# Four transformer-like layers on one core: operands of the scan's last batch, the order of two products, and where small steps are issued

## The chip, the cores and the metric

One core of one Trainium2 chip. The metric is the device time of one execution in microseconds (us). The engines are PE (matmul; its weight loads are shown as PEld), DVE (VectorE), ACT (ScalarE), POOL (GpSimd) and SP (SyncE, which here issues DMAs). Each takes its own instructions in order, and so do the DMA queues of SP, ACT and POOL in issuing.

## The reference, cut to what matters

The input is x of 4 batches x 512 tokens x 512 features, float32. Four layers follow each other, each added to x: causal attention, a ternary-weight FFN, a selective state-space scan, and a block of latent attention with a mixture of experts. The change touches the second stage (only in time: what runs between its products), the third, and the beginning of the fourth:

```python
# third layer, on the normed x; r = 128, n = 16 states, D = 512 features
xz = jnp.einsum('btd,rd->btr', x, W_xproj)
delta_r, B_mat, C_mat = xz[..., :r], xz[..., r:r + n], xz[..., r + n:]
delta = jax.nn.softplus(jnp.einsum('btr,dr->btd', delta_r, W_dt) + b_dt)
dA = jnp.exp(delta[..., None] * -jnp.exp(A_log))
Bu = delta[..., None] * B_mat[:, :, None, :] * x[..., None]
def step(h, inp):
    dA_t, Bu_t, C_t = inp
    h = dA_t * h + Bu_t
    return h, jnp.sum(h * C_t[:, None, :], axis=-1)
# fourth layer: the rmsnorm's weights ln1_w multiply the inputs of these three projections
kv_d, q_d, k_r = x @ kv_d_w, x @ q_d_w, x @ rope_k_w
```

## The kernel before, in words

The kernel goes through five stages: the first attention, the FFN (batches b = 0 to 3, eleven blocks f of hidden features each), the scan, the second attention, and the experts. Work of the next stage is cut into pieces by Python generators, and each `yield` ends a piece; the loop of the running stage calls `next` at fixed places, so the pieces lie between its own instructions.

**FFN.** PE's order is the order of the code; the other engines' order is set by a planner. `gated` (L819) makes the two hidden products of a block into a pair tile `pg` (two PSUM banks), ACT and DVE turn it into `sil`, `gh` and `gl`, and `down` (L837) multiplies back. Three pieces are called in each block, one of them between the two products of `gated`. In batches 1 to 3 these are pieces of `prepare(b - 1)`, which makes the inputs of the scan for the batch before: the projections `drT`, B and C, then in two halves the products with W_dt into a pair tile `pz` (L606), of which ACT takes the absolute value (`e`, L607) and DVE the positive part (`delta`, L608); then exponential, logarithm and sums, the store of `delta` to `deltas` and of delta times x, turned, to `dxs`, both in DRAM. Pair tiles have two buffers, single banks four.

**Scan.** Here the order of all five engines is the order of the code. There are 128 steps m over (batch, state n, half of the features), 32 steps a batch. In a step: `scale` (each second step) loads `diag` by SP and makes, by ACT, three rows `bu` (L1016) and four `da` (L1022) for the state after; `turn` brings the inputs into PSUM by PE (L1029, L1034) for the step after; `scan` is two DVE scans (L1042) into `h` (three buffers); `weigh` loads `cb` (L1050, three buffers) and POOL multiplies, `hc` (L1053); `add_up` sums three steps later on PE (L1066). `finish` adds a batch's sums to x at the third step of the batch after.

The scan's own inputs `delta_l` and `dxT` lie in the pool `large`, two buffers each, filled from DRAM by `fetch`: four pairs of SP loads, one pair a step. The inputs of the last batch are prepared during the scan by `prepare_last`, called at the first three steps and then at each second one; its tiles lie in a pool `c_p` on the right side of SBUF. It ends with, for each of four blocks k of features, ACT's copy of the product `pd` to `delta` (L738), its store to `deltas` (L739, ACT's queue), DVE's product with x (`ux`, L741), PE's turn `tpd` (L751), ACT's copy `st` (L734) and its store to `dxs` (L735, ACT's queue). The first block's copy is at step 67; at step 84 what is left is done at once, `c_p` is closed, and the pools `far` and `d_w` are opened in its place. Their first users at step 84 are SP's loads of `ln2` (L1121), `wr` (L1125) and `br` (L1127) and POOL's memset of `wr` (L1124). From step 84 `fetch(3)` loads the last batch, from 88 one weight of the second attention is loaded a step (eleven, L1134), and at steps 100, 102, 104 and 106 POOL multiplies a quarter of `wlat` and `wrk` by the norm's factors `ln1` (L1164; the profile calls wrk's tile `w_b`). Meanwhile `enter(0)` runs at every third step from 86: statistics of x by DVE (86 to 95), `shifted` and squares by ACT (L155, L915; 98 to 107), `root_inverse` (`ri_ln`, `ri_rms`: DVE L102, then POOL L103; 95 and 107), and rows and turns (110 to 125).

Of the kernel before, what the change touches and what calls it, by code (L numbers as in the profile page):

```python
# [11 lines left out]
F32 = mybir.dt.float32  # L12
# [3 lines left out]
ALU = mybir.AluOpType  # L16
# [30 lines left out]
def block_kernel(ctx: ExitStack, tc: tile.TileContext, a: dict, out: bass.AP):  # L47
# [24 lines left out]
    def by_tokens(x, b):  # L72
        return x[b * T : (b + 1) * T, :].rearrange("(t p) c -> p t c", p=P)

    def by_rows(w):
        return w.rearrange("(k p) o -> p k o", p=P)
# [420 lines left out]
    large = scans.enter_context(tc.tile_pool(name="large", bufs=2, reuse_waits="tile"))  # L497
    loaded = {}

    def fetch(b):  # L500

        delta = large.tile([P, NK, T], F32, tag="one", name="delta_l")
        dxT = large.tile([P, NT, C], F32, tag="two", name="dxT")
        loaded[b] = delta, dxT
        for i in range(NT):
            nc.sync.dma_start(dxT[:, i, :], by_tokens(dxs, b)[:, i, :])
            nc.sync.dma_start(delta[:, i, :], by_rows(deltas[b])[:, i, :])
            yield
# [45 lines left out]
    def prepare(b, pool, spot, spots, ahead):  # L554


        x = xs[b]
        uT = pool.tile([P, NK, T], F32, tag="uT", name="uT")
        ops, rows = [], {}
        layer_norm(pool, x, lambda t, op: ops.append(op))  # L560
        yield

        def make(t):
            row = rows[t] = pool.tile([P, C], F32, tag="row", name="row_s", bufs=ahead)
            ops[t](row)
            ud = pool.tile([P, C], F32, tag="u", name="ud")
            nc.gpsimd.tensor_tensor(ud, row, dpar, ALU.mult)
            nc.gpsimd.tensor_tensor(x[:, t, :], x[:, t, :], ud, ALU.add)

        make(0)  # L570
        make(1)
        yield
        for t in range(NT):
            transpose_into(uT, rows.pop(t), t * P, spot=spot)
            if t == 1:
                make(2)
                make(3)
            yield
        pd = spot("pd")
        for k in range(NK):  # L580
            nc.tensor.matmul(pd, wx[:, k, :RANK], uT[:, k, :], start=k == 0, stop=k == NK - 1)
            if k == 1:
                yield
        drT = pool.tile([P, T], F32, tag="drT", name="drT")
        nc.scalar.copy(drT, pd)
        yield
        pb = spot("pb")
        latents(pb, uT)
        bcT = pool.tile([P, P], F32, tag="bcT", name="bcT")
        nc.scalar.copy(bcT, pb[:, :P])  # L590
        keep_latents(b, bcT, nc.sync)
        yield
        pb = spot("pbt")
        nc.tensor.transpose(pb[:, :P], bcT, ident)
        e = pool.tile([P, NK, T], F32, tag="e", name="diag_s")
        nc.sync.dma_start(diags[b], keep_inputs(b, pb, e))
        yield
        yield


        delta = pool.tile([P, NK, T], F32, tag="delta", name="delta")
        e = pool.tile([P, NK, T], F32, tag="e", name="e")
        for half in range(2):
            for i, pz in enumerate(spots("pz")):
                k = 2 * half + i
                nc.tensor.matmul(pz, wdt[:, k * P : (k + 1) * P], drT, start=True, stop=True)  # L606
                nc.scalar.activation(e[:, k, :], pz, AF.Abs, bias=bdt[:, k : k + 1])  # L607
                nc.vector.tensor_scalar(delta[:, k, :], pz, bdt[:, k : k + 1], 0.0, ALU.add, ALU.max)  # L608
            yield half == 1
        nc.scalar.activation(e, e, AF.Exp, scale=-1.0)  # L610
        yield True
        for k in range(NK):
            u = pool.tile([P, T], F32, tag="u", name="u")
            nc.vector.tensor_scalar(u, e[:, k, :], 1.0, -1.0, ALU.add, ALU.add)
            nc.vector.tensor_tensor(u, e[:, k, :], u, ALU.subtract)
            nc.vector.tensor_tensor(delta[:, k, :], delta[:, k, :], u, ALU.add)
            yield True
        nc.scalar.activation(e, e, AF.Ln, bias=1.0)
        yield True
        scaled = {}  # L620

        def finish(k):
            nc.vector.tensor_tensor(delta[:, k, :], delta[:, k, :], e[:, k, :], ALU.add)
            nc.sync.dma_start(deltas[b, k * P : (k + 1) * P, :], delta[:, k, :])
            scaled[k] = pool.tile([P, T], F32, tag="ux", name="ux", bufs=2)
            nc.vector.tensor_tensor(scaled[k], delta[:, k, :], uT[:, k, :], ALU.mult)

        def turn_out(k):
            tp, ux = spot("tpd"), scaled.pop(k)
            for t in range(NT):  # L630
                nc.tensor.transpose(tp[:, t * P : (t + 1) * P], ux[:, t * P : (t + 1) * P], ident)
            st = pool.tile([P, NT, P], F32, tag="st", name="st")
            nc.scalar.copy(st.rearrange("p t q -> p (t q)"), tp)
            nc.sync.dma_start(by_tokens(dxs, b)[:, :, k * P : (k + 1) * P], st)

        finish(0)
        yield True
        finish(1)
        yield
        for k in range(NK):  # L640
            turn_out(k)
            if k + 2 < NK:
                yield True
                finish(k + 2)
            yield

    def prepare_last(b, pool):
# [70 lines left out]
        for t in range(NT + 1):  # L718
            if t > 0:
                nc.vector.tensor_tensor(x[:, t - 1, :], x[:, t - 1, :], y, ALU.add)  # L720
            if t < NT:
                y = bank("du")
                for k in range(NK):
                    nc.tensor.matmul(
                        y[:, k * P : (k + 1) * P], uT[:, k, t * P : (t + 1) * P], dd[:, k, :],
                        start=True, stop=True,
                    )
                yield
        terms = ((ident, relu), (ident, e), (minus, over), (ident, ln))
        scaled = tp = None  # L730
        for k in range(NK + 2):
            if k >= 2:
                st = pool.tile([P, NT, P], F32, tag="st", name="st")
                nc.scalar.copy(st.rearrange("p t q -> p (t q)"), tp)  # L734
                nc.scalar.dma_start(by_tokens(dxs, b)[:, :, (k - 2) * P : (k - 1) * P], st)  # L735
            if 1 <= k <= NK:
                delta = pool.tile([P, T], F32, tag="delta", name="delta", bufs=2)
                nc.scalar.copy(delta, pd)  # L738
                nc.scalar.dma_start(deltas[b, (k - 1) * P : k * P, :], delta)  # L739
                scaled = pool.tile([P, T], F32, tag="ux", name="ux", bufs=2)  # L740
                nc.vector.tensor_tensor(scaled, pd, uT[:, k - 1, :], ALU.mult)  # L741
            if k < NK:
                pd = bank("pdl")
                for i, (w, term) in enumerate(terms):
                    nc.tensor.matmul(pd, w, term[:, k, :], start=i == 0, stop=i == 3)
                    if i % 2 == 0:
                        yield
            if 1 <= k <= NK:
                tp = bank("tpd")
                for t in range(NT):  # L750
                    nc.tensor.transpose(tp[:, t * P : (t + 1) * P], scaled[:, t * P : (t + 1) * P], ident)  # L751
                yield
# [244 lines left out]
    with tc.tile_pool(name="c_1", bufs=1, reuse_waits="tile") as c1, tc.tile_pool(  # L997
# [83 lines left out]
        with tc.manual_schedule(engines=engines):  # L1081
# [4 lines left out]
            for m, (b, n, half) in enumerate(steps):  # L1086
# [27 lines left out]
                if m == 84:  # L1114
# [3 lines left out]

                    far = ctx.enter_context(tc.tile_pool(name="far", bufs=1, side="right"))
                    ln2 = far.tile([P, C], F32, tag="ln2", name="ln2")  # L1120
                    nc.sync.dma_start(ln2, a["ln2_w"].partition_broadcast(P))  # L1121

                    wr = far.tile([P, NK, RW], F32, tag="wr", name="wr")
                    nc.gpsimd.memset(wr, 0.0)  # L1124
                    nc.sync.dma_start(wr[:, :, :NR], by_rows(a["router_w"]))  # L1125
                    br = far.tile([P, NR], F32, tag="br", name="br")
                    nc.sync.dma_start(br, a["router_b"].partition_broadcast(P))  # L1127
                    logit = far.tile([P, TT, NR], F32, tag="logit", name="logit")

                    hs = [far.tile([P, NT, C], F32, tag=f"h{b}", name=f"h{b}") for b in range(B)]  # L1130
# [22 lines left out]
                    cos1 = held("cos1", [P, NT, RD], a["cos1"].rearrange("(t p) d -> p t d", p=P))  # L1153
                    sin1 = held("sin1", [P, NT, RD], a["sin1"].rearrange("(t p) d -> p t d", p=P))
                    wow = held("wow", [P, NK, C], by_rows(a["o_w"]))
                    coming = fetch(B - 1)
                if m >= 84:
                    next(coming, None)
                if m >= 88 and loads:
                    loads.pop(0)()  # L1160
                if 100 <= m < 100 + 2 * NK and m % 2 == 0:
                    k = (m - 100) // 2
                    for w in (wlat[:, k].rearrange("p i r -> p (i r)"), wrk[:, k]):
                        nc.gpsimd.tensor_scalar(w, w, ln1[:, k : k + 1], None, ALU.mult)  # L1164
            for step in steps[-3:]:
                add_up(*step)
            finish(B - 1)
# [569 lines left out]
```

## Time and profile before

| | us |
|---|---|
| median of 3 runs | 1910.6 (1908.81 to 1911.85) |
| profiled execution | 1912.04 |
| its span, first to last instruction | 1910.3 |
| mean granted TensorE clock | 0.980 |
| FFN, about | 480 to 753 |
| scan, first to last scan instruction | 755.3 to 1109.1 |

In the profile a line names engine, line of the kernel, operation and tiles (written <- read). Times are counted from the first instruction. An entry in brackets at the end of a timeline line is the idle time of the engine before it and what ended that; a group's last numbers are busy time and the mean of one in ns. One step of the scan starts its POOL product at 757.7 us (step 0), 985.65 (84), 1032.7 (98) and 1111.6 (127).

### The profile page before, as it was taken

What the parts mean: (1) busy time and instruction counts of PE and PEld (TensorE: products, weight loads), DVE (VectorE), ACT (ScalarE), POOL (GpSimd) and SP (SyncE); (2) the same over time, 40 slices, a digit from 0 to 9 for tenths busy, and PEclk for the clock granted to TensorE, in tenths of its full rate; (3) what the DMA queues carried; (4) which work ended last, traced back from release to release, by engine and by line L of the source; (5) the groups of instructions that cost most, each with busy time, mean ns of one, the idle gap of its engine ahead of it and who ended that gap; (6) DMA issues with size and microseconds to landing.
All of it is one profiled execution on the core that took longest, in us unless ns stands there. A gap on an engine that the chain in (4) does not pass through costs nothing. (4 is left out here: it accounts for less than half of the span.)

```text
span 1910.3 us, 27470 instructions
## 1 busy us (share of the span) xinstructions
PE 1767.4 (93%) x10374; PEld 1089.5 (57%) x10374; DVE 1119.4 (59%) x1812; ACT 937.5 (49%) x1932; POOL 575.0 (30%) x391
## 2 busy tenths in 40 slices
PE   7999999999999988988988888999999999999998
PEld 3433343437766666878877764555555554554444
DVE  6456445656564636998979856475565663422222
ACT  2433433333242436989977956566676662111111
POOL 2221212120202020989868940100001000144431
PEclk9999999999999999999999988999999999999999
DMA  7002200102010202332234200000001005545545
GB/s 250 8 1 89 82 1 1 45 1 78 1 56 34 89 23 78 96 112 81 70 127 125 62 6 1 1 10 14 1 23 34 23 7 179 196 89 89 93 81 139
DMA packets 78470, 119.27 MB, mean 62 GB/s; under 512 B 9802, under 2 KB 37066, under 8 KB 77780
## 3 DMA queue, kind: packets, MB, share of 16 engines
q1 hardware_dynamic: 66148, 92.97, 15.1%
q0 software_dynamic: 8656, 20.32, 6.0%
q10 hardware_dynamic: 3536, 4.23, 0.7%
q8 instruction: 83, 1.36, 0.3%
q14 instruction: 47, 0.39, 0.1%
HBM read 85.12 MB, written 35.52 MB: 63 GB/s over the span
## 5 line engine op out<-in xcount | busy, mean ns | idle before, releaser
L1053 POOL TENSOR_TENSOR hc<-h,cb 128x1024 f32<-128x1024 f32 x128 | 301.1, 2406 | 112.6 <-DVE h L1042 94.1
L1042 DVE TENSOR_TENSOR_SCAN h<-da,bu 128x512 f32<-128x512 f32 x256 | 291.2, 1199 | 26.1 <-PE bu L1034 13.1
L284 PE MATMUL pq<-wqkv,hT 128*128 128x512 f32 x384 | 179.4, 615 | 1.8 <-ACT hT L133 1.8
L1022 ACT ACTIVATE da<-delta_l,am 128x511 f32<-128x511 f32 x256 | 163.9, 709 | 6.7 <-DVE h L1042 6.7
L1314 ACT ACTIVATE pr<-scd,nm 128x128 f32<-128x128 f32 (+3 forms) x256 | 133.2, 528 | 56.1 <-DVE nm L1311 53.5
L819 PE MATMUL pg<-hTh,w 128*128 128x512 f32 (+1 forms) x352 | 146.3, 416 | 2.4 <-DVE sil L825 1.7
L1066 PE MATMUL ys<-ident,hc 128*128 128x128 f32 x1024 | 138.6, 279 | 6.9 <-POOL hc L1053 4.0
L819 PE MATMUL pg<-hTl,w 128*128 128x512 f32 (+1 forms) x352 | 140.1, 398 | 0.2 <-DVE hTl L807 0.2
L1034 PE MATMUL bu<-ident,bu 128*128 128x128 f32 x768 | 133.2, 281 | 7.5 <-ACT bu L1016 7.5
L1616 PE MATMUL pgr<-wgu,gTe 128*128 x304 | 137.1, 593 | 0.0
L1016 ACT ACTIVATE bu<-dxT,bts 128x512 f32<-128x512 f32 x192 | 124.3, 711 | 23.1 <-PE bu L1034 21.2
L1029 PE MATMUL bu<-diag_l,dxT 128*128 128x128 f32 x512 | 108.7, 295 | 27.1 <-DVE h L1042 15.3
L364 ACT ACTIVATE pt<-sc 128x1024 f32<-128x1024 f32 (+3 forms) x128 | 84.1, 698 | 85.0 <-PE sc L359 82.6
L284 PEld LDWEIGHTS pq<-wqkv,hT 128*128 128x128 f32 x384 | 71.4, 194 | 94.4 <-issue 84.8
L1066 PEld LDWEIGHTS ys<-ident,hc 128*128 128x128 f32 x1024 | 119.7, 144 | 9.5 <-POOL hc L1053 5.9
L1303 PE MATMUL scd<-qkTd 32*128 32x512 f32 (+3 forms) x512 | 106.9, 496 | 13.7 <-ACT pr L1314 12.7
L1029 PEld LDWEIGHTS bu<-diag_l,dxT 128*128 128x128 f32 x512 | 81.3, 198 | 48.1 <-DVE h L1042 26.9
L1311 DVE TENSOR_REDUCE nm<-scd 128x2 f32<-128x256 f32 (+3 forms) x128 | 104.2, 815 | 0.0
L1326 PEld LDWEIGHTS tpd<-ident,pr 128*128 128x128 f32 x640 | 68.8, 142 | 60.2 <-issue 41.6
L1034 PEld LDWEIGHTS bu<-ident,bu 128*128 128x128 f32 x768 | 96.5, 146 | 11.5 <-ACT bu L1016 11.4
L365 POOL TENSOR_SCALAR_AFFINE_SELECT pt<-pt 128x512 f32<-128x512 f32 x64 | 43.5, 679 | 197.0 <-ACT pt L364 197.0
L1326 PE MATMUL tpd<-ident,pr 128*128 128x128 f32 x640 | 100.3, 288 | 0.6 <-ACT pr L1314 0.6
(310 smaller groups left out, 3184.9 us busy)
## 6 DMA issues: line engine op xcount, KB each, us to landing
cb<-c_rows SPq DMA_DIRECT2D x64, 256.0 KB, 3.1
q_w<-in_w2T SPq DMA_DIRECT2D x20, 256.0 KB, 2.8
delta_l<-deltas SPq DMA_DIRECT2D x16, 256.0 KB, 3.6
dxT<-dxs SPq DMA_DIRECT2D x16, 256.0 KB, 4.2
diag_l<-diags SPq DMA_DIRECT2D x64, 64.0 KB, 1.9
hrows<-h SPq DMA_DIRECT2D x4, 1024.0 KB, 4.6
acc<-x SPq DMA_DIRECT2D x16, 256.0 KB, 2.0
wgu<-in_r_gate SPq DMA_DIRECT2D x7, 512.0 KB, 9.6
```

Of the source, the lines that this page charges most:

```text
L284: nc.tensor.matmul(y, inputs_T[b][:, k, t * P : (t + 1) * P], wqkv[:, k, s * C : (s + 1) * C], start=k == 0, stop=k == NK - 1,)
L819: nc.tensor.matmul(pg[:rows, i, :], w[:, k, f * P : f * P + rows], part[:, k, :], start=k + m == 0, stop=k + m == NK,)
L1016: nc.scalar.activation(row, dxT[:, t, :], AF.Copy, scale=bts[:, b, t * NS + n : t * NS + n + 1])
L1022: nc.scalar.activation(da[:, k, 1:], delta[:, k, 1:], AF.Exp, scale=am[:, k, n : n + 1])
L1029: nc.tensor.matmul(bu[:, :P], loaded[b][1][:, 0, k * P : (k + 1) * P], scaled[b, n][0], start=True, stop=True,)
L1034: nc.tensor.transpose(bu[:, t * P : (t + 1) * P], scaled[b, n][t][:, k * P : (k + 1) * P], ident)
L1042: nc.vector.tensor_tensor_scan(h[:, i, :], decays[b, n][:, 2 * half + i, :], bu, 0.0, ALU.mult, ALU.add)
L1053: nc.gpsimd.tensor_tensor(hc, states.pop((b, n, half)), weighed[b, n].unsqueeze(1).to_broadcast([P, 2, T]), ALU.mult)
L1066: nc.tensor.matmul(sums[b][t][:, k * P : (k + 1) * P], hc[:, i, t * P : (t + 1) * P], ident, is_transpose=True, start=n == 0 and k == 0, s ...
L1314: nc.scalar.activation(pr[:, i, :w], sc[:, i, :w], AF.Exp, bias=nm[:, i : i + 1], accum_out=sums[b, g][:, t, 2 * p + i : 2 * p + i + 1],)
L1326: nc.tensor.transpose(tp[:, j * P : (j + 1) * P], pr[:, i, j * P : (j + 1) * P], ident)
L1616: nc.tensor.matmul(pg, gT[:, k, :], wgu[:, bass.ds(e, 1), k, :].rearrange("p e o -> p (e o)"), start=k == 0, stop=k == NK - 1,)
```

## The change

1. In `prepare` the two products of a half are both issued before the two readers of each.
2. `fetch` is split: `places` allots the tiles `delta_l` and `dxT` of a batch. `prepare_last` allots them for the last batch, and ACT copies `pd` and `tpd` into them. The tiles `delta` and `st`, the eight stores on ACT's queue and `fetch(3)` with its eight loads on SP are dropped.
3. At step 84 nothing is loaded or cleared any more: `ln2`, `wr` (with its memset) and `br` come at the end of the list of weights, which is taken one a step from step 86 on (fifteen entries).
4. The products by `ln1` go from POOL (steps 100 to 106) to ACT (steps 104 to 110).

```diff
-    def fetch(b):
-
+    def places(b):
         delta = large.tile([P, NK, T], F32, tag="one", name="delta_l")
         dxT = large.tile([P, NT, C], F32, tag="two", name="dxT")
         loaded[b] = delta, dxT
+        return loaded[b]
+
+    def fetch(b):
+
+        delta, dxT = places(b)
         for i in range(NT):
...
         for half in range(2):
-            for i, pz in enumerate(spots("pz")):
+            both = spots("pz")
+            for i, pz in enumerate(both):
                 k = 2 * half + i
                 nc.tensor.matmul(pz, wdt[:, k * P : (k + 1) * P], drT, start=True, stop=True)
+            for i, pz in enumerate(both):
+                k = 2 * half + i
                 nc.scalar.activation(e[:, k, :], pz, AF.Abs, bias=bdt[:, k : k + 1])
                 nc.vector.tensor_scalar(delta[:, k, :], pz, bdt[:, k : k + 1], 0.0, ALU.add, ALU.max)
...
+        delta, dxT = places(b)
         terms = ((ident, relu), (ident, e), (minus, over), (ident, ln))
         scaled = tp = None
         for k in range(NK + 2):
             if k >= 2:
-                st = pool.tile([P, NT, P], F32, tag="st", name="st")
-                nc.scalar.copy(st.rearrange("p t q -> p (t q)"), tp)
-                nc.scalar.dma_start(by_tokens(dxs, b)[:, :, (k - 2) * P : (k - 1) * P], st)
+                nc.scalar.copy(
+                    dxT[:, :, (k - 2) * P : (k - 1) * P], tp.rearrange("p (t q) -> p t q", t=NT)
+                )
             if 1 <= k <= NK:
-                delta = pool.tile([P, T], F32, tag="delta", name="delta", bufs=2)
-                nc.scalar.copy(delta, pd)
-                nc.scalar.dma_start(deltas[b, (k - 1) * P : k * P, :], delta)
+                nc.scalar.copy(delta[:, k - 1, :], pd)
...
                     ln2 = far.tile([P, C], F32, tag="ln2", name="ln2")
-                    nc.sync.dma_start(ln2, a["ln2_w"].partition_broadcast(P))
...
-                    nc.gpsimd.memset(wr, 0.0)
-                    nc.sync.dma_start(wr[:, :, :NR], by_rows(a["router_w"]))
...
-                    nc.sync.dma_start(br, a["router_b"].partition_broadcast(P))
...
                     wow = held("wow", [P, NK, C], by_rows(a["o_w"]))
-                    coming = fetch(B - 1)
-                if m >= 84:
-                    next(coming, None)
-                if m >= 88 and loads:
+                    hold(ln2, a["ln2_w"].partition_broadcast(P))
+                    loads.append(lambda: nc.gpsimd.memset(wr, 0.0))
+                    hold(wr[:, :, :NR], by_rows(a["router_w"]))
+                    hold(br, a["router_b"].partition_broadcast(P))
+                if m >= 86 and loads:
                     loads.pop(0)()
-                if 100 <= m < 100 + 2 * NK and m % 2 == 0:
-                    k = (m - 100) // 2
+                if 104 <= m < 104 + 2 * NK and m % 2 == 0:
+                    k = (m - 104) // 2
                     for w in (wlat[:, k].rearrange("p i r -> p (i r)"), wrk[:, k]):
-                        nc.gpsimd.tensor_scalar(w, w, ln1[:, k : k + 1], None, ALU.mult)
+                        nc.scalar.activation(w, w, AF.Copy, scale=ln1[:, k : k + 1])
```

## Prediction

> **What bounds the kernel now.** I read the page first, then the waits, then the timeline around each edited line.
>
> ```profile
> PE 1767.4 (93%) x10374; PEld 1089.5 (57%) x10374; DVE 1119.4 (59%) x1812; ACT 937.5 (49%) x1932; POOL 575.0 (30%) x391
> ...
> PE   7999999999999988988988888999999999999998
> ...
> DVE  6456445656564636998979856475565663422222
> ...
> POOL 2221212120202020989868940100001000144431
> ```
>
> A slice is 47.8 us. The FFN (slices 10 to 15) is PE's: 9 beside 6 or less elsewhere. In the scan (slices 15 to 23) POOL and DVE stand at 8 and 9, so a step there goes at the pace of one of them until a wait intervenes. The printed chain of waits begins at 1114 us, behind both stages; each is therefore read from its own waits.
>
> In PE's waits between 480 and 753 us (total, times, longest) the first line is the edited one; the timeline shows one occurrence:
>
> ```profile
> PE pz L606 <- DVE delta L608: 11.5, 6, 3.5
> ```
> ```profile
> 533.82 1.02 PE L606 MATMUL pz<-drT,wdt 128*128 128x512 f32 x2
> 534.97 0.69 ACT L607 ACTIVATE e<-pz,bdt 128x512 f32<-128x512 f32 x1 [2.46 <-DMA diags<-diag_s]
> 535.69 0.75 DVE L608 TENSOR_SCALAR delta<-pz,bdt 128x512 f32<-128x512 f32 x1 [2.46 <-ACT e L607]
> 536.49 1.12 PE L606 MATMUL pz<-drT,wdt 128*128 128x512 f32 x2 [1.65 <-DVE delta L608]
> ```
>
> The second product of a pair starts when both readers of the first are done, though it writes the other bank: a pair tile is guarded as a whole. In the scan one wait of SyncE's queue stands out, and the timeline (step 84 is at 985 us) shows what it starts:
>
> ```profile
> SPq L1121 <- DMA dxs<-st: 15.5, 1, 15.5
> ```
> ```profile
> 991.49 0.33 SPq L1121 DMA_DIRECT2D ln<-in_ln_w  x1
> 991.56 0.21 POOL L1124 MEMSET wr<- 128x128 f32 x1 [3.55 <-DMA dxs<-st]
> ...
> 994.79 0.43 SPq L1012 DMA_DIRECT2D diag_l<-diags  x1
> 995.26 0.43 SPq L1050 DMA_DIRECT2D cb<-c_rows  x1
> ...
> 999.95 0.76 PE L1029 MATMUL bu<-diag_l,dxT 128*128 128x128 f32 x2 [7.87 <-DMA diag_l<-diags]
> ...
> 1000.61 4.67 POOL L1053 TENSOR_TENSOR hc<-h,cb 128x1024 f32<-128x1024 f32 x2 [6.53 <-DMA cb<-c_rows]
> ```
>
> SP and POOL both wait for the last store of the preparation to land, since ln2 and wr lie in its memory; the scan's own loads queue behind and come late.
>
> **The change, part by part.** The sum is made against the profiled execution: 1912.0 us, span 1910.3, 1.4 over the median of 1910.6. Gains are positive.
>
> *Both products first (FFN, batches 1 to 3).* PE then issues two products (0.43 each) and the eight matmuls behind (0.23 each): from 533.82 to 537.4. The readers still take turns: ACT's copy of one half of a pair waits for DVE's read of the other half in the waits (ACT qkd L975 <- DVE qkd L986: 11.3 us, 12 times). So 0.69 + 0.75 + 0.69 + 0.75 and four hand-overs of 0.04 make 3.0 us, from 535.6 to 538.6. The second half's tile takes the first one's buffer: its first matmul, at 539.32, comes just behind the last reader (538.38 + 0.75) while the other pair buffer is still being read by sil, at 539.58. So a wait of 1.3 us (537.4 to 538.7) stays in place of 1.65, and the 1.56 of the second half goes. Next come two products and eight L837: the next pg starts at 542.2 instead of 544.70, 2.45 earlier; a wait of 0.74 on sil at 551.6 shrinks a little. I take 2.6 for each of batches 1 and 2. In batch 3 the first reader waits for the diags store until 703.2 and PE idles 3.52; afterwards PE runs at half pace (0.43 between L819 matmuls) until 708.5, about 1.5 lost. After the change PE goes on with pg and meets its wait at the second half, 703.8 to 706.2; it is at 707.9 instead of 712.36. The table load, Exp and table load (1.28 + 1.92 + 1.28) behind the last reader then hold sil and gh until 717.6, where PE waits some 2.3 instead of 0.3: 3.3 remain. Sum 8.5. Below: if the second half takes pg's buffer, it waits for sil and L825 as well, until 539.4: 5. Above: all six idles, the slow clock and restarts: 13.4. It can't fall below nothing, as PE gets no new instruction and ACT and DVE have idle time here.
>
> [...] If 2.4 slowed PE as 3.52 did, the sum would be up to 1.5 smaller.
>
> *Last batch in SBUF.* Eight ACT DMA issues go (four each at L735 and L739, steps 67 to 85), and eight SP loads of 256 KB. The copies stay, 0.56 and 0.59, with another destination.
>
> ```profile
> 952.71 0.59 ACT L738 COPY delta<-pdl 128x512 f32<-128x512 f32 x1 [0.45 <-ACT st L734]
> ...
> 953.33 0.69 DVE L741 TENSOR_TENSOR ux<-pdl,uT 128x512 f32<-128x512 f32 x1 [1.22 <-ACT delta L738]
> ```
>
> Three times (steps 73, 79, 85) the 0.45 of an issue stands ahead of the copy for which DVE waits: 1.3. The other five issues are hidden, since ACT waits 0.3 to 1.3 for PE's bu two rows further on. Bounds 0 and 8 x 0.45 = 3.6. The new writes wait for batch 1's readers, which end at step 63; the first copy is at 67.
>
> *No wait at step 84.* hc of step 85 starts at 991.73 and that of 86 at 1000.61, where two steps later the pace is 2.33. Without the wait, hc 85 follows DVE's scan of 85 (989.7), hc 86 that of 86 (992.8), hc 87 and 88 POOL's 2.34 (995.1, 997.5), and the scan of 89 ends at 1000.4, with the statistics' 0.85 ahead of it: hc 89 at 1000.5 instead of 1008.66. That is 8.1, and as DVE is then the later engine up to step 94 it is kept. Bounds 6, and 10.3 (both delays less one 2.34 step each). What could be late next: the first load (ln1, step 86) still waits for the preparation's last reader, PE's turn at 988.1, and behind it on SP stand step 90's diag and step 88's cb, out by 989.5 and wanted at 997; these 7 us cover it. One load a step is 0.4 to 0.5 of SP, which is idle. The memset (0.21) goes to step 98 on POOL, and wr's load behind it holds SP until then. Diag for 102 and cb for 100 go out at 1036 (in times of before), landing in 1.9 and 3.1 us, where they are wanted at 1038.3 and 1039.7: cost 0 to 1.5, hidden by DVE's four adds at step 99 (2.45) and POOL's idle time at 107. I take 0.
>
> *The norm's factors.*
>
> ```profile
> 1054.99 0.95 POOL L1164 TENSOR_SCALAR wlat<-wlat,ln 128x256 f32<-128x256 f32 x1
> 1055.89 0.95 POOL L1164 TENSOR_SCALAR w_b<-w_b,ln 128x256 f32<-128x256 f32 x1
> ...
> 1057.78 3.73 DVE L102 TENSOR_SCALAR ri_rms<-ss_d 128x4 f32<-128x4 f32 x1 [2.72 <-ACT sq_d L915]
> ```
>
> POOL loses four pairs, 4 x 1.8 = 7.2. ACT gains eight of 128x256: a 512 row from SBUF goes every 0.64 (bu, three in 1.94), and a 128x256 copy is 0.22 shorter than a 128x512 one (372 and 592 ns from PSUM): 0.42 each, 3.4 in all. ACT is without a gap from 1030.4 to 1057.7, where ri_rms waits for its last square; two pairs (steps 104, 106) stand ahead of that square and make it 1.7 later, 59.45. But ri_rms, 3.73 here and 0.17 elsewhere, ends with POOL's second queued hc; POOL will have caught up by then. The scan of 107 starts at 59.6 instead of 1061.43. From 107 on POOL runs without a gap to the end (2.34 a step) and ACT keeps ahead. Gain 2.1 with hand-overs. Bounds -3.4 (all of ACT's work on the path) and 7.2; I stay near the row that decides, ri_rms.
>
> [...]
>
> Sum: 8.5 + 1.3 + 8.1 + 2.1 = 20.0; 1910.6 - 20.0 = 1890.6.
>
> **The rivals.** (a) *The FFN waits go altogether* (halves read apart): 13.4 there, 24.9 in all, 1885.7. For: different banks. Against: the sil activation starts only when both halves of pg are written. (b) *ACT becomes the scan's bound*: the square at 107 is late and an hc is under way when ri_rms starts, so that it waits up to 2.3 more, and the later pairs (108, 110) delay da. The last part costs up to 3 instead of gaining 2.1: 15 in all, 1895.6. For: ACT's gapless 27 us. Against: POOL's lead after 107. [...] (c) *The FFN wait only moves* to the second half's buffer and to gh: 1 instead of 8.5 there, 1898.1. For: the 3.0 chain is longer than PE's eight matmuls (1.9). (d) *Slower*: the weights' loads, now ACT's to wait for, land after ACT reaches step 104; being in order, ACT then holds bu and da, and the scan stands still one us for each us. It decides from 24 us behind step 104, which makes 1914.4 and more. Against: these loads (steps 86 to 89) landed 4.4 us after issue before, some 38 us ahead of use.
>
> **How the numbers follow.** Forecast 0.50 (its own range 1887 to 1895), (a) 0.14, (b) 0.16, (c) 0.14, no change 0.03, (d) 0.03. About 0.2%, 3.8 us, is what a measurement can tell. The range from 1884 to 1899 holds the forecast, (b), (c) and most of (a). Faster 0.94, same 0.03, slower 0.03.
>
> **What would show it.** PE's wait on delta L608 gone, with one of some 1.3 us (2.4 in batch 3) on the second half; no wait of SP or POOL on dxs; POOL steps at 84 to 90 under 3.1; ri_rms near 0.2, at step 107. Wrong would be: PE waits over 2 us at every second half, or POOL steps over 2.4 after 107 with DVE waiting for da.

## The result, and the profile after

After: 1908.0 us, the median of 20 runs; before: 1913.3, of as many on the same chips. One of the 20 runs of after took 2504.8 us at a granted clock of 0.65 and is left out of the ratio. The ratio is 0.9967 (0.9955 to 0.9978), so the change saves 6.3 us (4.2 to 8.6) where 20.0 were forecast. The profiled execution of after took 1909.5 us, its span 1907.8.

The page of after, in the rows that were shown of before, and the row of the granted clock, of after and then of before:

```profile
PE 1779.0 (93%) x10374; PEld 1099.5 (58%) x10374; DVE 1115.1 (58%) x1812; ACT 940.0 (49%) x1940; POOL 568.5 (30%) x383
...
PE   7999999999999898998998979999999999999998
...
DVE  6456445656555646899998946475666653422222
...
POOL 2221212120202020879888930100001000144431
PEclk9999999999999999999999987999999989999999
```
```profile
PEclk9999999999999999999999988999999999999999
```

POOL has lost its eight products by the norm's factors (391 to 383 instructions) and ACT has gained them (1932 to 1940). PE is busy 11.6 us longer with the same 10374 matmuls: more of them ran at the slow clock (0.973 granted on average, 0.980 before).

**FFN.** PE's waits between 480 and 756 us in after, and then the line of before that answers to the first:

```profile
PE tpd L638 <- DVE ux L633: 6.8, 3, 2.4
PE pz L611 <- DVE delta L615: 4.7, 3, 2.3
```
```profile
PE tpd L631 <- DVE ux L626: 1.2, 2, 0.6
```

The wait of the edited line fell from 11.5 to 4.7, as forecast (1.3 + 1.3 + 2.4). The wait of the transposes tpd for ux, the product that the same chain ends in, rose from 1.2 to 6.8. The timeline of batch 1 shows both ends of that chain:

```profile
534.78 1.88 PE L611 MATMUL pz<-drT,wdt 128*128 128x512 f32 x4
...
538.93 0.75 DVE L615 TENSOR_SCALAR delta<-pz,bdt 128x512 f32<-128x512 f32 x1 [0.75 <-ACT e L614]
...
539.74 1.55 PE L611 MATMUL pz<-drT,wdt 128*128 128x512 f32 x3 [1.22 <-DVE delta L615]
```
```profile
561.71 1.29 DVE L633 TENSOR_TENSOR ux<-delta,uT 128x512 f32<-128x512 f32 x2
...
562.54 0.63 PE L638 MATMUL tpd<-ident,ux 128*128 128x128 f32 x4 [2.19 <-DVE ux L633]
...
562.92 0.63 PE L843 MATMUL y<-w,gh 128*128 128x512 f32 x1
...
563.36 0.63 PE L843 MATMUL y<-w,gl 128*128 128x512 f32 x1
```

Counted from the first pz, PE is ready for tpd after 25.6 us instead of 27.8, but the transposes start after 27.8 instead of 28.4: of 2.2 us gained, 0.65 are left. Then the y matmuls come every 0.43 us instead of 0.23, up to 566: this wait was followed by 3.4 us of half clock (granted 0.50). So PE's gain is spent in two ways. The waits that this view lists between 480 and 756 us fell only from 23.6 to 20.4 in all, and the half clock between the first pg and the scan's first bu (the scan's first product) rose from 7.7 to 17.1 us. That second part is partly chance: over five profiles each, the means are 6.7 and 11.6, and the ranges overlap (0.0 to 11.3, 3.4 to 17.1).

**Scan.** The timeline of after at steps 84 to 89 and at step 107:

```profile
986.14 2.36 POOL L1059 TENSOR_TENSOR hc<-h,cb 128x1024 f32<-128x1024 f32 x1 [0.52 <-POOL hc L1059]
...
988.10 0.38 SPq L1136 DMA_DIRECT2D ln<-in_ln_w  x1
...
989.74 2.39 POOL L1059 TENSOR_TENSOR hc<-h,cb 128x1024 f32<-128x1024 f32 x1 [1.24 <-DVE h L1048]
...
992.76 7.05 POOL L1059 TENSOR_TENSOR hc<-h,cb 128x1024 f32<-128x1024 f32 x3 [0.63 <-POOL hc L1059]
...
1000.27 2.38 POOL L1059 TENSOR_TENSOR hc<-h,cb 128x1024 f32<-128x1024 f32 x1 [0.46 <-DVE h L1048]
```
```profile
1048.57 0.49 ACT L1167 ACTIVATE wlat<-wlat,ln 128x256 f32<-128x256 f32 x1
1048.97 0.49 ACT L1167 ACTIVATE w_b<-w_b,ln 128x256 f32<-128x256 f32 x1
1050.19 0.63 ACT L921 ACTIVATE sq_d<-h 128x512 f32<-128x512 f32 x1
...
1050.95 0.17 DVE L102 TENSOR_SCALAR ri_rms<-ss_d 128x4 f32<-128x4 f32 x1 [6.65 <-ACT sq_d L921]
1051.03 3.44 DVE L1048 TENSOR_TENSOR_SCAN h<-da,bu 128x512 f32<-128x512 f32 x3
```

Steps 85 to 89 start where the forecast put them (989.7, 992.8, 995.1, 997.5, 1000.5). ri_rms is down from 3.73 to 0.17 and waits for its square, which two pairs of factors precede. The scan of step 107 starts at 1051.0 instead of 1061.4.

**Behind the scan**, in code that the change leaves alone, time is given back. From the last hc to the first scd, before and then after (columns: window, its length, busy time of PE, PEld, DVE, ACT and POOL, then the granted clock):

```profile
1111.58:1151.67 40.09, 31.95 (x119) 20.19 (x119) 18.36 (x59) 21.24 (x43) 11.48 (x10) 0.88 0.00 0
```
```profile
1101.00:1142.80 41.80, 32.87 (x120) 20.53 (x117) 18.36 (x59) 21.44 (x43) 11.47 (x10) 0.84 0.00 0
```

The same work on DVE, ACT and POOL, 1.7 us more, a lower clock. (scd is the first product of the second attention; pge, below, the first of the experts.)

### The profile page after: what moved, and what is told of

It is laid out like the page before. It is cut to its first block, busy times and chain, and to the rows that moved or that the text cites. A ratio compares the mean times of both kernels' runs of the same rounds, so it can differ in the third digit from the quotient of the medians.

```text
span 1907.8 us, 27483 instructions
## 1 busy us (share of the span) xinstructions
PE 1779.0 (93%) x10374; PEld 1099.5 (58%) x10374; DVE 1115.1 (58%) x1812; ACT 940.0 (49%) x1940; POOL 568.5 (30%) x383
## 5 line engine op out<-in xcount | busy, mean ns | idle before, releaser
L1329 PE MATMUL tpd<-ident,pr 128*128 128x128 f32 x640 | 104.8, 297 | 0.6 <-ACT pr L1317 0.6
L1035 PEld LDWEIGHTS bu<-diag_l,dxT 128*128 128x128 f32 x512 | 80.8, 196 | 37.8 <-DVE h L1048 25.6
## 6 DMA issues: line engine op xcount, KB each, us to landing
wgu<-in_r_up SPq DMA_DIRECT2D x7, 512.0 KB, 10.2
```

The lines of the kernel that those rows point to most:

```text
L1035: nc.tensor.matmul(bu[:, :P], loaded[b][1][:, 0, k * P : (k + 1) * P], scaled[b, n][0], start=True, stop=True,)
L1329: nc.tensor.transpose(tp[:, j * P : (j + 1) * P], pr[:, i, j * P : (j + 1) * P], ident)
```

## The experiments

Each comparison is with the kernel before on the same chip. The stages named are read from PE's and POOL's positions in each profile; all of them stand in the table at the end of this section.

**A control: the kernel before, unchanged.**

> The kernel before, unchanged, as a control: ratio 1.000. What it is for is the stretch behind the scan, whose code neither kernel changes: from the first scd to the end it took 758.7 us in the profile of before and 765.0 in that of after, and 34 us of it ran at half clock in after against 17 in before (at its start). Theory A (half-clock windows come by chance there, run by run): this second profile of the same program differs from 758.7 by some us, and the runs' mean clocks spread over 0.97 to 0.98. Theory B (the change itself brings the windows on): 758.7 again within 1 us, clocks near 0.980 where those of after lay at 0.971 to 0.977.

Ratio 1.000 (0.9976 to 1.0023). The second attention took 436.6 us with 37.5 of it at half clock, against 429.3 and 17.1 in the first profile. The mean clocks of before's runs on that chip reach from 0.967 to 0.980 with the program unchanged. Theory A holds there: the 765.0 of after against the 758.7 of before behind the first scd, in the first two profiles, is within what before does by itself (766.0 here); the profile that the forecast was worked from has the shortest second attention of the five with the old scan.

**The FFN part alone.**

```
-            for i, pz in enumerate(spots("pz")):
+            both = spots("pz")
+            for i, pz in enumerate(both):
                 ... the product
+            for i, pz in enumerate(both):
                 ... the two readers
```

> The kernel before with the FFN's part of the change alone (both W_dt products first). The sum of the prediction, 8.5: about 1904.8 against 1913.3, ratio 0.9956. Theory that the wait moves on: the readers of the second half end when they ended before, so Exp, Ln, ux and the transposes tpd come no earlier; PE's wait for delta shrinks from 11.5 to about 4.8 us in all, and its waits for ux at tpd grow by 1.5 in each batch, from the 0.6 of before to some 2.2; the FFN's end stays within 1 us of 752 and the time at 0 to 2 us less, ratio 0.999 to 1.000. By the theory that a half-clock window then comes at tpd (562.5 in after) at random, the gain differs by 1.5 us from batch to batch.

1914.9 us, ratio 0.9994 (0.9977 to 1.0011). PE's waits are those of after to the digit: 6.8 at tpd for ux, 4.7 at pz. The stretch from the first pg to the first bu took 318.6. The theory that the wait moves on holds, the sum's 8.5 does not.

**The scan's parts alone** (after, with the FFN loop of before).

> The kernel after without the FFN's part: the last batch's inputs in SBUF, loads one a step, norm's factors by ScalarE. If the FFN part is worth nothing: the ratio of after, 0.9967 (0.9955 to 0.9978), that is 6 us less; if it is worth 8.5 and the rest lost elsewhere: slower than before by 2 us. In the profile, the scan ends 10 to 11 us earlier than in before whatever else holds (from turn 0 to the last hc 360.2 before, 350.1 after). Theory A (windows by chance behind the scan): the second attention lasts 756 to 767. Theory B (the scan's parts bring them on): 764 to 766 again.

1912.4, ratio 0.9983 (0.9964 to 1.0002). The scan took 346.4 from the first bu to the last hc, 11.5 less than the 357.8 of before; the second attention 432.3. The total is short of what the stage gained, and its interval is too wide to say by how much.

**SBUF and loads alone** (as the last, with the factors back on GpSimd at steps 100 to 106).

> The kernel before with the last batch's inputs kept in SBUF and the loads moved, but the norm's factors still multiplied by GpSimd (steps 100 to 106) and the FFN as before. By the prediction's terms 1.3 + 8.1 = 9.4 us of the scan's gain: scan 351 instead of 360.2, and the norm's factors would be the 2 us that separate it from the run without the FFN part. If the norm's factors are worth more (POOL loses 7.2 us to them): the scan ends at 355 or later. Total: ratio 0.995 if all of it reaches the end, 0.997 to 0.998 if the stretch behind loses 4.

1910.5, ratio 0.9969 (0.9949 to 0.9990). The scan took 348.9, 8.9 under before: the terms 1.3 and 8.1 together, within half a microsecond.

**tpd one part later.** If the wait only moved along the chain, giving the chain time should bring the gain. In `prepare` of the kernel after:

```
         finish(1)
         yield
+        yield True
         for k in range(NK):
             turn_out(k)
```

> The kernel after with the transposes tpd of the preparation (L638) put one part later in the FFN's order, in each of the batches 1 to 3, so that a group of pg or y stands on PE between the last ux and its reader. Theory that the FFN's gain went into the wait at tpd: PE's waits there (tpd <- ux: 6.8 us in 3, in after) fall under 1 us, PE's idle of the edited chain stays at the 4.7 of pz, and the stretch from the first pg to the scan's first bu, 318.6 to 320.7 in the two profiles with the FFN part, comes to 313 to 316; total 4 to 6 us under after. Rival: the wait moves on once more, to pg or y, which wait for sil behind Ln and a table load on ACT (Silu ended at 562.5 where ux did, in after): the stretch stays at 318 to 321 and the total within 1 us of after.

1899.0, ratio 0.9900 (0.9869 to 0.9931). PE's waits in the same stretch as above:

```profile
PE pz L611 <- DVE delta L615: 4.7, 3, 2.3
...
PE tpd L638 <- DVE sil L832: 2.2, 2, 1.1
...
PE tpd L638 <- DVE ux L633: 0.5, 1, 0.5
```

The stretch from the first pg to the first bu is 309.9, lower than was expected. 6.8 of waiting became 2.7; the rest is partly a draw of the clock, as 4 us of the stage ran at half clock here and 0 to 11 in the six profiles with this edit. The profiles without any half clock in the stage leave the clock out of the comparison: 317.0 us with the FFN of before (one profile), 310.2 and 311.1 with both edits.

**The same edit without the products first, and with them on the old scan.**

> The kernel before with the transposes tpd one part later and nothing else (no product moved). There PE waits 1.2 us for ux and 1.3 for sil at tpd in all. Theory that the earlier products and the later transposes need each other: 0 to 3 us under before, the stretch from the first pg to the scan's first bu stays at 318 to 322. Rival, that the later transposes alone made the 9 us seen when they were put on the kernel after: the stretch falls to 310 to 313 here too. As a further profile with the old scan: from the last hc to the first scd 39.9 to 40.1 again, if the scan's form fixes the place of the half-clock windows.

> The kernel before with both parts in the FFN, the products first and tpd one part later; the scan as in before. The stretch from the first pg to the first bu at 309 to 312 (309.9 and 311.1 with the new scan), the total 8 to 11 us under before, ratio 0.9945 to 0.996. The last hc to the first scd 39.9 to 40.1 if the old scan fixes the windows' place, 41.3 to 41.9 if chance does.

Later transposes alone: 1915.3, ratio 0.9998 (0.9978 to 1.0017), stretch 318.8; PE still waits 11.5 at pz. Both: 1907.7, ratio 0.9955 (0.9934 to 0.9976), stretch 310.2. So each edit alone is worth nothing that these runs can tell, and both together 8.6 us. There were two waits for one chain: with the products first alone, PE loses the time at tpd; with the later transposes alone, the 11.5 at pz stand and there was little to open at tpd (1.2). From the last hc to the first scd both profiles took 39.8 to 40.1 again, as expected if the scan's form fixes it.

**The norm's factors by themselves.** The kernel with tpd later, with the factors on GpSimd again:

> The kernel after with tpd one part later, and the norm's factors multiplied by GpSimd again in steps 100 to 106: the term of ScalarE's factors by itself, as the base is 345.3 to 345.8 us from the first bu to the last hc. By the prediction 2.1 us more, 347.5 to 348; by POOL's 7.2 us of products 352; if ScalarE were the scan's bound, no more than 345.

1901.4, ratio 0.9937 (0.9912 to 0.9963). The scan took 349.6 against 345.3 to 347.7 with ScalarE's factors: 2 to 4 us, nearest to the forecast's 2.1 among the three; the 7.2 of POOL's products isn't it.

**Dummy products around the scan's end.** To see whether half clock costs the time behind the scan, PE was given products that nobody reads in its gaps there, first too many:

```
+    def warm(n):
+        to = bank("warm")
+        for _ in range(n):
+            nc.tensor.matmul(to, ident, warmer[0][:, 0, :], start=True, stop=True)
```

> The kernel after with products of ident and v_u_w into banks that nobody reads, put into PE's gaps around the scan's end: 2, 3 and 3 ahead of the last three add-ups, 4 behind, 3 and 6 ahead of the first and the last transposes of qkd, 4 ahead of the third scd (0.43 us each at full clock). Theory that the time behind the scan was lost to half-clock windows which PE's gaps start: the windows at 1102 (10.2 us) and 1140 (27.3 us) go or shrink to a few us; pl takes 7 instead of 9.7, the last hc to the first scd 38 to 39 instead of 41.8, and the second attention 423 to 430 instead of 432 to 435; total 6 to 12 under after. Rival, that the windows follow from the attention's own narrow products (32 rows): they stay at 27 us, and the total stays or rises by the dummies that don't fit, 1 to 3 us.

> The kernel after, unchanged, on the same chip as the other two, as their base and for a second profile: ratio 0.9967 (0.9955 to 0.9978). If the half-clock windows behind the scan come by chance: the stretch from the first scd to pge between 429 and 437 with 17 to 38 us of half clock. If the earlier end of the scan fixes their place: the last hc to the first scd 41.8 again (39.9 to 40.1 in the three profiles with the old scan), a window of 27 us that begins ahead of the first scd.

> The two edits together, tpd one part later and the dummy products at the scan's end, on the kernel after. If both theories hold the gains add: 10 to 18 us under after, 1890 to 1898. If neither does: within 2 us of after.

1906.5 (0.9943, 0.9920 to 0.9965) beside 1910.4 of after unchanged (0.9958, 0.9936 to 0.9980), and 1901.2 with tpd later (0.9906, 0.9878 to 0.9933), no better than without. The half clock from the last hc to the first scd went from 13.1 us to nothing, but the stretch grew to 44.7: each dummy takes 0.86 us, two passes of 0.43, not the 0.43 that was reckoned, and what didn't fit delayed pl and the transposes. (The prediction's "two products (0.43 each)" are four such passes too; its 537.4 counts four.) The expectation was wrong in its price, and so inconclusive on the cause. After unchanged took 41.3 us from the last hc to the first scd again and had the half-clock stretch of 27.3 us from ahead of the first scd, so the scan's end, not chance alone, sets that place. With dummies that fit (0, 1 and 2 ahead of the last three add-ups, 2 behind, 1 and 3 ahead of qkd's transposes, 2 ahead of the third scd):

> The kernel after with tpd one part later and with dummy products that fit the gaps (each takes 0.86 us, not 0.43): 0, 1 and 2 ahead of the last three add-ups, 2 behind them, 1 and 3 ahead of the first and last transposes of qkd, 2 ahead of the third scd. Theory that half-clock windows at the scan's end cost time that can be had back: from the last hc to the first scd 38 to 39 instead of 41.8, with no half clock in it; the second attention 429 to 435; total 3 to 5 us under the same kernel without dummies (1899.0 in its runs), about 1895. Rival, that the windows come elsewhere instead: total unchanged within 2 us.

> The kernel after with the fitted dummy products around the scan's end and nothing else. If the half-clock windows make the 1.8 us there: from the last hc to the first scd 38.3 to 38.5, as in the run with the later transposes; total 3 to 5 us under after. If something else does: over 39, total less than 2 us under after.

> The kernel before with the same dummy products. If the half-clock windows make the difference of 1.8: the same 38.3 to 38.5 from the last hc to the first scd as on the new scan, that is 1.6 less than the 40.0 of the old scan; total 1 to 4 us under before. If another cause makes it: 36.5, 1.8 less than with the new scan.

> The kernel after with tpd one part later, without dummies, once more on the same chip as the others: ratio 0.990 (0.987 to 0.993), some 8 to 11 us under after; the stretch from the first pg to the first bu 309 to 313; from the last hc to the first scd 41.3 to 42.0 again.

With tpd later: 1891.0, ratio 0.9871 (0.9837 to 0.9905), the best version run. On after alone: 1897.8 (0.9905, 0.9877 to 0.9933). On before: 1912.2 (0.9985, 0.9966 to 1.0004). The base, tpd later without dummies: 1897.8 (0.9906, 0.9879 to 0.9933). The stretch from the last hc to the first scd, on the new scan and then on the old one:

```profile
1098.53:1136.87 38.34, 35.36 (x135) 20.86 (x132) 18.37 (x59) 21.23 (x43) 11.47 (x10) 1.00 0.00 1
```
```profile
1107.35:1145.71 38.36, 35.36 (x136) 20.87 (x133) 18.38 (x59) 21.29 (x43) 11.48 (x10) 1.00 0.00 1
```

Without half clock both scans take the same 38.3, so the 1.7 us that the new scan loses there go with the half clock. The amount alone doesn't set it: after and tpd later, each run again, had 9.7 and 9.5 us of half clock there and took 41.3 and 41.4, and before took 40.1 with 9.9, so it counts where the half clock falls. With the dummies PE is busy for 35.4 of the 38.3 us, so a small difference of another kind could be hidden; that is not excluded. With the dummies in both kernels the change is worth 1912.2 - 1897.8 = 14.4 us between the medians, instead of 5.3 (1913.3 - 1908.0, on other chips). On after they gave more than the 3 to 5 us that were expected: a ratio of 0.9905 where after had 0.9967 and 0.9958, some 10 to 12 us.

The stages over all profiles, in us, with the number of profiles:

| stage | code of before | code of after | other |
|---|---|---|---|
| first pg to first bu | 317.0 to 322.7, mean 320.4 (5) | 316.3 to 321.9, mean 319.0 (5) | tpd later too: 309.9 to 312.7, mean 311.3 (6) |
| first bu to last hc | 357.5 to 359.3, mean 358.4 (6) | 345.3 to 347.7, mean 346.4 (9) | factors on GpSimd: 348.9, 349.6 |
| last hc to first scd | 39.8 to 40.1 (5) | 41.3 to 42.0 (7) | fitted dummies: 38.3 to 38.4 (3) |
| first scd to pge | 429.3 to 438.3, mean 433.7 (5) | 432.3 to 435.5, mean 434.2 (7) | fitted dummies: 427.9 to 429.7 (3) |

## Why the prediction was wrong

**Both products first: the failed step.** The local part came as worked out. Behind the first pz the second half started after 4.96 us (forecast 4.88), with a wait of 1.22 (1.3); the next pg after 8.6 (8.4; 10.9 before); batch 3 waited 2.28 (2.4). Wrong was "I take 2.6 for each of batches 1 and 2", and the 3.3 of batch 3 with it: the gain was read off at the next pg and carried to the end of the stage. Nothing was asked of the chain behind the second readers (Exp, three operations of DVE a slice, Ln, ux, each with FFN work between), whose end PE meets 23 us later at tpd. That chain hardly moved: the readers of a half still take four turns after one another, and the last of the second half starts 9.21 us behind the first pz instead of 9.97, while PE's next pg gained 2.3. Before and then after:

```profile
543.79 0.75 DVE L608 TENSOR_SCALAR delta<-pz,bdt 128x512 f32<-128x512 f32 x1 [1.34 <-ACT e L607]
```
```profile
543.99 0.75 DVE L615 TENSOR_SCALAR delta<-pz,bdt 128x512 f32<-128x512 f32 x1 [0.76 <-ACT e L614]
```

Of these 0.76 us, 0.65 reached tpd. The term was 8.5 and measures 1.4 between the stage's means; the run of it alone gives 1.1 (-2.1 to 4.4). Rival (c) had this size (1) and named another place, the second half's buffer and gh. A slip in the sum is small beside this: "some 2.3 instead of 0.3" in batch 3 leaves 2.5, and 3.3 only with both waits of before, 0.33 on gh and 0.78 on gl; in after 0.32 was waited there, and then 2.40 at tpd.

**Last batch in SBUF and no wait at step 84: right.** 1.3 + 8.1 = 9.4 were forecast; 358.4 - 349.3 = 9.1 came. At steps 73 and 79 the interval from the hc before went from 4.15 to 3.60, 0.55 each instead of 0.45; at 85 it went from 6.08 to 3.60, where the stall of step 84 is in it too. (The sign "POOL steps at 84 to 90 under 3.1" was set too low for this one: the forecast's own times, 985.65 and 989.7, give 4.05.) Of what could be late next, the memset held SP for wr as foreseen,

```profile
SPq L1136 <- POOL wr L1159: 13.9, 1, 13.9
```

and POOL then waited 0.45 us for cb at 1031.7, which step 107 absorbs.

**The norm's factors: right, a little small.** 2.1 forecast, 349.3 - 346.4 = 2.9 measured. The factor is 0.49 us long, one every 0.40 (0.42 forecast). Rivals (b) and (d) didn't happen: DVE's wait for da fell from 6.7 to 6.0 us, and ri_rms, which in before ended 0.04 us behind the second of two hc (1061.51 and 1061.47), met none in after (1050.95; POOL's last hc had ended at 1048.08). Nor did (a): 4.7 us of waiting at pz are left.

**Nothing was priced behind the scan.** 20.0 was taken to reach the end. 1.7 us of it is lost between the last hc and the first scd, in seven profiles out of seven. The second attention's means differ by 0.5 with ranges that overlap, so no loss is shown there. The experts behind, which the table leaves out, took 328.7 to 329.6 us from pge to the end in five profiles with the old scan and 328.7 to 333.9 in seven with the new one, 0.9 more in the mean; in two of the seven 6.8 us of half clock fell there. 1.4 + 12.0 - 1.7 - 0.5 - 0.9 is 10.3, more than the 6.3 and the 8.1 (0.0042 of 1918.2, for after run again) of the ratios. The rest isn't placed. One thing points to the clock: on the chip where after was run again, it had a mean of 0.9729 and before 0.9752, though after no longer has the 10.2 us of half clock that lay in and behind the stall at step 84 (995.2 to 1005.4, PE busy for 5.5 of it). Between the shortest and the longest second attention with the old scan, 27.3 us more of half clock went with 9.0 us more of time, a third (429.3 us with 17.1 of it, 438.3 with 44.4).

**The clock.** The sum lets PE run at full clock behind the 2.4 us that it waits in batch 3. That was the author's assumption, which no run had shown: in before, 3.52 us of idle time were followed by the 0.43 pace and 1.65 by 0.23. The runs then bore it out in six profiles of eleven. In after, the 2.28 us of batch 3 are followed by half clock. Two stretches around the restart, in after and then in the kernel with both FFN edits on the old scan:

```profile
703.00:706.40 3.40, 1.12 (x6) 0.59 (x4) 1.50 (x2) 1.37 (x2) 0.00 (x0) 1.00 0.00 0
706.40:709.80 3.40, 3.40 (x5) 1.32 (x5) 0.00 (x0) 0.00 (x0) 0.00 (x0) 0.51 0.00 0
```
```profile
698.00:702.00 4.00, 1.72 (x6) 0.80 (x5) 1.50 (x2) 1.21 (x2) 0.00 (x0) 1.00 0.00 0
702.00:706.00 4.00, 4.00 (x17) 2.89 (x17) 1.63 (x3) 2.27 (x4) 0.00 (x0) 1.00 0.00 0
```

The same idle of 2.28 to 2.30 us stands in eleven profiles; in five the four passes behind it were slowed (2.5 to 3.7 us), in six not (2.0). The price is thus 0.5 to 1.7 us where it comes, near the "up to 1.5" that was allowed for.

## What to carry to other kernels

A wait that is removed is gone only if nothing later waits for the same chain: follow the chain from the removed wait to the next place where the bounding engine meets it, and move that place too. Here each of two edits was worth nothing that the runs could tell, and both together 8.6 us. Price a stage's end by what follows it: where the granted clock differs between kernels in one stage (0.88 in before, 0.84 in after and 1.00 with the fitted dummies from the last hc to the first scd: 40.1, 41.8 and 38.3 us), a stage that ends elsewhere can cost or gain time in code that nobody touched, 1.7 us here, and a profile's total holds one draw of it; several profiles of the same program show how wide that is.

## What the hardware showed unexpectedly

In these profiles half-clock stretches (granted 0.50) start on a grid. In before the next six starts lie 8, 53, 141, 153, 167 and 171 times 3.413 us behind the first one (182.8 us), within 0.06 us, and their lengths are whole multiples of it; the grid's place differs from run to run (the start near 182 us lies at 180.1 to 184.2). With each profile's grid carried on from its half-clock starts, the eleven idles of 2.28 to 2.30 us part cleanly by where they fall: in the five that were followed by half clock, 2.02 to 2.30 us of the idle fell into one window of the grid, the 3.413 us between two of its lines; in the six others no window had more than 1.90 of it.

In after a half-clock stretch outlasted the idle time by far: PE idled 3.30 us until 1140.90 and 2.08 until 1145.68, and the clock stayed at 0.50 until 1167.2, while PE was shown busy for 20.4 of the last 20.5 us. A part of it, at the start of the second attention, with products of 32 rows and transposes:

```profile
1150.00:1160.00 10.00, 10.00 (x52) 4.70 (x50) 5.58 (x10) 4.79 (x16) 0.00 (x0) 0.50 0.00 0
```

The stretch lasted 27.3 us, from ahead of the first scd, and 17.1 in before. With the fitted dummies ahead, it was 10.2 to 13.7 and began 6 to 7 us behind the first scd. The old scan's end meets the grid at another place than the new one's in every profile. The grid's place is a matter of chance only when it is counted from the kernel's start; counted from the grid itself, the last hc starts 0.3 to 0.9 us behind a line of it in all six profiles with the old scan and 1.5 to 2.5 us behind one in all eleven with the new. That would fit the new scan's length: 12.0 us less is three and a half windows of 3.413 us. How a kernel that starts anywhere on the grid comes to keep its place on it stays open.
